# One norm moved ahead of a masking, and five small steps two units later, in a cross-attention and FFN kernel

## The chip, the cores and the metric

The kernel runs on one core of a Trainium2 chip. The metric is the device time of one execution in microseconds (us), lower is better. Engines are called as in the profile: PE (TensorE's matmuls), PEld (its weight loads), DVE (VectorE), ACT (ScalarE), POOL (GpSimd), SP (SyncE, which here only issues DMAs).

## The reference

What is computed, cut to what matters (one batch, 2048 tokens of width 256, a context of 1601 rows of width 192, 16 heads of width 64, one extra "null" key and value):

```python
x = x + _L0_xattn_ref(_layernorm(x, axis=-1), ctx_768, mask, g_norm, null_kv, Wq, Wkv, Wout, g_out)
x = x + _L0_ffn_ref(_layernorm(x, axis=-1), k0, k1, k2, s0, s1, s2)

def _L0_xattn_ref(x, context, mask, g_norm, null_kv, Wq, Wkv, Wout, g_out):
    q = layer_norm(x, g_norm) @ Wq
    k, v = jnp.split(context @ Wkv, 2, axis=-1)
    # 16 heads; null key and value in front; masked softmax; weighted values
    out = softmax(where(mask, (q * s) @ (k * s).T, -max)) @ v
    return layer_norm(out @ Wout, g_out)

def _L0_ffn_ref(x, k0, k1, k2, s0, s1, s2):
    h = s0 * (concat([x, -x]) @ where(k0, 1.0, -1.0))
    h = s1 * ((relu(h) * 2) @ where(k1, 1.0, -1.0))
    return s2 * ((relu(h) * 2) @ where(k2, 1.0, -1.0))
```

The signs and sizes of the scalars s0, s1, s2 are folded into the FFN's weights and its last scale.

## The kernel before, in words

The 2048 tokens are four blocks of 512 (`b`), the 16 heads are eight pairs (`p`). The attention is a list of 32 units `u`, one for each pair and block, pairs outermost; unit 0 is pair 0 with block 0, unit 1 is pair 0 with block 1. Everything is issued in the written order (a manual schedule): each engine takes its instructions in the order of the code, and waits by semaphore for what others make.

A unit has this course, with the names that the profile shows:

- A loop over 13 chunks of 128 keys (`KC`). For each, PE computes the scores `sT` (L393; L404 adds the shift for the first two), ACT makes the exponentials `e` (L406), and POOL adds them up in `acc` (L621, L623). In the same loop PE makes a chunk of coarse scores for the *next* unit, `max` (L356, L340), from `qr` and `kr`, and DVE takes its maximum, `mx` (L359, L343). `max` lies in the two PSUM buffers called flex (`ps_f`), so a chunk can be computed only when the maximum before the last one has been taken. `sT`, `av` and `po` use the two others (`ps_s`).
- At the loop's end DVE combines the maxima in `mcol` (L364).
- PE computes the weighted values `av` (L413) over the same 13 chunks. Behind its third chunk comes `divided` for the unit before: PE sums `acc` over the keys (`den`, L431), DVE takes the reciprocal and multiplies (`aoT`, L433 and L434).
- Behind it, in this order: ACT copies `av` to `avs` (L671); `max_turned` turns `mcol` on PE and makes the shift `mT` on DVE (L369, L371); `project_out` for the unit before (PE `po` L421, then DVE into `y_sb`, L424 or L426); `project_q` for the unit after next (`psq` L213, then `qr` and `qT` on ACT); and a part of the next pair's keys or values (`psk` L238 and L243, `kT` on ACT L249, `kr` on DVE L250; or `psv`).

In the first two units there is more. The input norm of blocks 0 and 1 is done ahead of unit 0; that of blocks 2 and 3 inside units 0 and 1. It has two parts. `input_root` and `input_normed` take the statistics of four tiles on DVE (L77, L78), the root on ACT (L443), the reciprocal (L447) and the negated mean `nm` (L140) on DVE, and then eight steps on ACT (L143, L144) into `y_sb`; behind them one ACT step loads the table for the exponentials again (`warm`). After `av`, `input_turned` turns the result on PE (`xT`, L458) and scales it into `xnT`, one half on ACT (L459), one on DVE (L463). `project_q` for unit 2 reads `xnT` of block 2.

In unit 0 only there are two further pieces, both on DVE. The first is the masking of the context: `ctx_a` and `ctx_b`, 128 x 1602 each, are multiplied by `keep` (L641), after an SP DMA has filled the lower half of `ctx_b` (L639). The first readers of the masked context are the `psk` matmuls at the end of unit 0. The second is the signs: five steps on tiles of one or two columns (L665 to L669) that make `sgn`, the absolute scales and `s_out`. `sgn` is read four units from the end, where the FFN's first weights `w0` are made (L655, L657), and `s_out` in the FFN.

POOL's sums and ACT's exponentials are tied by two one-element copies on ACT: `seen` (L608, L611). The second, ahead of a unit's third exponential, waits for the last `acc` of the unit before, and POOL's first sum of a unit stands behind it.

Of the kernel before, what the change touches and what calls it, by code (L numbers as in the profile page):

```python
# [12 lines left out]
AF = mybir.ActivationFunctionType  # L13
# [23 lines left out]
def xattn_ffn(ctx, tc, x, ctxT, mask, g_norm, null_kv, wq, wkv, wout, g_out, k0, k1, k2, s0, s1, s2, out):  # L37
    nc = tc.nc
# [20 lines left out]
    eps_sb = cp.tile([128, 1], F32, name="eps_sb")  # L59
# [8 lines left out]
    warm = cp.tile([128, 1], F32, name="warm")  # L68

    def stats(src, n, name, mv=None):  # L70

        at = 0 if mv is None else 2
        if mv is None:
            mv = sp.tile([128, 4, 2], F32, tag="mv", name=f"mv_{name}")
        for j in range(n):
            st = sp.tile([128, 6], F32, tag="st", name=f"st_{name}_{at + j}")
            nc.vector.bn_stats(st, src[:, j, :])  # L77
            nc.vector.bn_aggr(mv[:, at + j, :], st)  # L78
        return mv
# [8 lines left out]
    def centred(dst, src, mv, r, j):  # L88
        nc.vector.tensor_scalar(dst, src, mv[:, j, 0:1], r[:, j : j + 1], ALU.subtract, ALU.mult)  # L89
# [10 lines left out]
    def norm_begin(b, src, name):  # L100

        mv = stats(src[:, ts(b, 4), :], 4, f"{name}{b}")
        r = sp.tile([128, 4], F32, tag="rstd", name=f"rstd_{name}{b}")
        norms[b] = (mv, r)

    def norm_root(b):
        mv, r = norms[b]
        nc.scalar.activation(r, mv[:, :, 1], AF.Sqrt, bias=eps_sb)

    def norm_end(b, dst, src, beside=False):  # L110
        mv, r = norms[b]
        nc.vector.reciprocal(r, r)
        if beside:
            centred_beside(dst, src, mv, r, b)
            return
        for j in range(4 * b, 4 * b + 4):
            centred(dst[:, j, :], src[:, j, :], mv, r, j - 4 * b)
# [19 lines left out]
    def centred_beside(dst, src, mv, r, b):  # L137

        nm = sp.tile([128, 4], F32, tag="nm", name=f"nm_{b}_{n_slots}")
        nc.vector.tensor_scalar(nm, mv[:, :, 0], -1.0, None, ALU.mult)  # L140
        for j in range(4):
            t = 4 * b + j
            nc.scalar.activation(dst[:, t, :], src[:, t, :], AF.Identity, bias=nm[:, j : j + 1])  # L143
            nc.scalar.mul(dst[:, t, :], dst[:, t, :], r[:, j : j + 1])  # L144

    with ExitStack() as att:
# [293 lines left out]
        def input_root(b):  # L440
            mv = stats(x_sb[:, ts(b, 4), :], 4, f"x{b}")
            r = sp.tile([128, 4], F32, tag="rstd", name=f"rstd_x{b}")
            nc.scalar.activation(r, mv[:, :, 1], AF.Sqrt, bias=eps2_sb, scale=1.0 + EPS)  # L443
            return mv, r

        def input_normed(b, mv, r, beside=False):
            nc.vector.reciprocal(r, r)  # L447
            if beside:
                centred_beside(y_sb, x_sb, mv, r, b)
                return  # L450
            for j in range(4):
                centred(y_sb[:, 4 * b + j, :], x_sb[:, 4 * b + j, :], mv, r, j)
# [127 lines left out]
        with tc.manual_schedule():  # L580
            for u, (p, b) in enumerate(units):
# [48 lines left out]
                if u == len(units) - 2:  # L630
                    norm_begin(0, y_sb, "y")
                    norm_root(0)
                    norm_end(0, y_sb, y_sb, beside=True)

                    nc.scalar.activation(warm, eps_sb, AF.Exp)
                if u == 0:


                    nc.sync.dma_start(out=ctx_b[64:, 1:], in_=ctxT[128:CD, :])  # L639
                    for part in (ctx_a, ctx_b):  # L640
                        nc.vector.tensor_tensor(part, part, keep, ALU.mult)  # L641
                if u < 2:
                    input_normed(u + 2, *input_root(u + 2), beside=True)
                    nc.scalar.activation(warm, eps_sb, AF.Exp)

                av = spare(f"av_{p}_{b}")
                for k in range(KC):
# [3 lines left out]
                if u in (len(units) - 4, len(units) - 3):  # L651
# [4 lines left out]
                    else:  # L656
# [2 lines left out]
                        )  # L659
                        nc.vector.tensor_scalar_mul(s1b[:, 0:1], sgn[:, 1:2], 2.0)  # L660
                        nc.vector.tensor_scalar_mul(s1b[:, 1:2], sgn[:, 1:2], -1.0)
                if u == 0:


                    nc.vector.tensor_scalar(sgn, s_sb[:, 0:2], 0.0, None, ALU.is_ge)  # L665
                    nc.vector.tensor_scalar(sgn, sgn, 2.0, -1.0, ALU.mult, ALU.add)
                    nc.vector.tensor_tensor(s_sb[:, 0:2], s_sb[:, 0:2], sgn, ALU.mult)
                    nc.vector.tensor_scalar(s_out, s_sb[:, 0:1], s_sb[:, 1:2], 8.0, ALU.mult, ALU.mult)
                    nc.vector.tensor_tensor(s_out, s_out, s_sb[:, 2:3], ALU.mult)  # L669
# [166 lines left out]
```

## Time and profile before

| | |
|---|---|
| Median of 3 runs | 1310.03 us (1309.79 to 1311.21) |
| Profiled execution | 1309.9 us, span 1308.1 us, mean granted clock 0.996 |
| PE busy | 1290.2 us, 99% of the span |
| DVE busy | 819.7 us, 63% |
| ACT busy | 624.7 us, 48% |
| POOL busy | 997.9 us, 76% |
| Costliest group | POOL `acc` L623, 352 sums, 847.0 us |
| Unit 0's loop begins, unit 1's, unit 2's | about 39, 80.8, 115.4 us |

The span counts from the first to the last instruction. The granted clock is the share of TensorE's full speed that the chip allowed. A duration in the trace includes the time for which an instruction was held after it was issued, so that the same operation can have rows of different length. "Idle before" is the time for which an engine had nothing running ahead of an instruction, with what ended it.

### The profile page before, as it was taken

Reading aid. Unit: us, or ns where it says so; the run is one execution under the profiler, and the core shown is the slowest. Engines: PE = TensorE matmul, PEld = TensorE weight load, DVE = VectorE, ACT = ScalarE, POOL = GpSimd, SP = SyncE. Lnnn points to the kernel's source line nnn. Section 1 sums busy time; section 2 is a strip of 40 time slices with the busy share of each in tenths; the row PEclk is TensorE's granted clock in tenths of the full one; section 3 lists DMA queues with packets and bytes.
Section 4 is the critical chain, followed back from the end, with each engine's and each line's share of the span. In section 5 each row is a group of like instructions: output and inputs, shape, how many; then the busy total and the mean of one; then the engine's idle time right before and its main releaser. Section 6 shows DMA issues by size and latency. Waiting matters only on the chain.

```text
span 1308.1 us, 15963 instructions
## 1 busy us (share of the span) xinstructions
PE 1290.2 (99%) x6568; PEld 657.8 (50%) x6568; DVE 819.7 (63%) x822; ACT 624.7 (48%) x740; POOL 997.9 (76%) x503
## 2 busy tenths in 40 slices
PE   8989999999999999999999999999999999999998
PEld 6334444444444444444444444444444443688887
DVE  7877666666666666666666666666666784554431
ACT  4576444444444444454555555555555457321121
POOL 4768988898889888998889888988898999611100
PEclk9989999999999999999999999999999999999999
DMA  6100000000000000000000000000000010000000
GB/s 143 21 1 5 1 1 13 6 1 1 13 5 1 1 13 5 1 1 5 9 5 1 1 13 5 1 1 5 1 17 1 1 41 1 1 9 9 17 17 17
DMA packets 16122, 13.18 MB, mean 10 GB/s; under 512 B 2656, under 2 KB 15520, under 8 KB 16048
## 3 DMA queue, kind: packets, MB, share of 16 engines
q1 hardware_dynamic: 14928, 11.02, 3.2%
q8 instruction: 52, 0.85, 0.3%
q10 hardware_dynamic: 640, 0.79, 0.2%
q0 software_dynamic: 480, 0.34, 0.2%
q14 instruction: 22, 0.18, 0.0%
HBM read 10.04 MB, written 2.10 MB: 9 GB/s over the span
## 4 chain that ended last, share of the span: by engine, by line
PE 91%; DVE 3%; ACT 2%; POOL 2%; DMA 1%; issue 1%; SPq 0%; DVEq 0%; POOLq 0%; ACTq 0%
PE sT L393 28%; PE av L413 26%; PE ps L720 9%; PE max L356 7%; PE psq L213 4%; PE po L421 4%; PE ps L746 2%; PE den L431 2%; PE psv L298 2%; PE psk L238 2%; PE sT L404 1%; DVE mx L359 1%; POOL acc L623 1%; PE psv L310 1%; DMA x_sb<-in_x 1%; PE psk L243 1%
## 5 line engine op out<-in xcount | busy, mean ns | idle before, releaser
L623 POOL TENSOR_TENSOR acc<-acc,e 128x1024 f32<-128x1024 f32 (+1 forms) x352 | 847.0, 2406 | 27.6
L359 DVE TENSOR_REDUCE mx<-max 128x2 f32<-128x1024 f32 x384 | 452.0, 1221 | 81.4 <-PE max L356 81.3
L406 ACT ACTIVATE e<-sT,maskb 128x1024 f32<-128x1024 f32 (+1 forms) x416 | 459.6, 1113 | 42.0 <-PE sT L404 11.8
L393 PE MATMUL sT<-qT,kT 64*128 64x512 f32 (+1 forms) x1664 | 448.5, 612 | 0.8 <-ACT e L406 0.2
L413 PE MATMUL av<-e,v 128*64 128x512 f32 (+1 forms) x1664 | 369.5, 594 | 0.2 <-ACT e L406 0.2
L356 PE MATMUL max<-kr,qr 64*128 64x512 f32 x768 | 292.4, 750 | 0.0
L413 PEld LDWEIGHTS av<-e,v 128*64 128x64 f32 (+1 forms) x1664 | 116.7, 137 | 237.7 <-issue 222.6
L393 PEld LDWEIGHTS sT<-qT,kT 64*128 64x128 f32 (+1 forms) x1664 | 130.4, 181 | 153.6 <-ACT e L406 144.3
L671 ACT COPY avs<-av 128x512 f32<-128x512 f32 x32 | 18.7, 585 | 321.6 <-PE av L413 321.6
L433 DVE RECIPROCAL aoT<-den 128x512 f32<-128x512 f32 x31 | 104.0, 3356 | 60.0 <-PE den L431 60.0
L621 POOL TENSOR_TENSOR acc<-e,e 128x1024 f32<-128x1024 f32 x32 | 75.6, 2362 | 70.1 <-ACT seen L611 58.4
L356 PEld LDWEIGHTS max<-kr,qr 64*128 64x128 f32 x768 | 76.1, 187 | 90.4 <-DVE mx L359 68.4
L371 DVE TENSOR_TENSOR mT<-mt,pick 128x512 fp32r<-128x512 f32 x32 | 22.1, 691 | 119.0 <-PE mt L369 119.0
L720 PE MATMUL ps<-h0hi,w 128*128 128x512 f32 x256 | 79.6, 392 | 0.1
L720 PE MATMUL ps<-h0lo,w 128*128 128x512 f32 x256 | 78.9, 389 | 0.0
L122 POOL TENSOR_TENSOR y_sb<-y_sb,gout_sb 128x256 f32<-128x256 f32 x12 | 9.3, 776 | 88.8 <-DVE y_sb L89 88.8
L214 ACT ACTIVATE qr<-psq 128x512 fp32r<-128x512 f32 x32 | 19.1, 597 | 100.0 <-PE psq L213 97.1
L213 PE MATMUL psq<-xnT,wq 128*128 128x512 f32 x124 | 60.2, 609 | 2.5 <-DVE xnT L463 2.5
L709 DVE SCALAR_TENSOR_TENSOR h1lo<-ps,h1hi 128x1024 fp32r<-128x1024 f32 x16 | 19.6, 1224 | 68.3 <-ACT h1hi L708 68.2
L708 ACT ACTIVATE h1hi<-ps 128x1024 fp32r<-128x1024 f32 x16 | 16.4, 1025 | 95.0 <-PE ps L720 95.0
L421 PE MATMUL po<-wo,aoT 128*128 128x256 f32 x256 | 60.6, 379 | 0.0
L404 PE MATMUL sT<-mT,ones_r 64*128 64x512 f32 x128 | 52.3, 787 | 1.3 <-DVE mT L371 1.3
(157 smaller groups left out, 1060.9 us busy)
## 6 DMA issues: line engine op xcount, KB each, us to landing
out_x<-o SPq DMA_DIRECT2D x7, 256.0 KB, 2.1
x_sb<-in_x SPq DMA_DIRECT2D x3, 512.0 KB, 8.2
wa<-in_wkv SPq DMA_DIRECT2D x8, 128.0 KB, 2.7
wq<-in_wq SPq DMA_DIRECT2D x8, 128.0 KB, 2.2
wo<-in_wout SPq DMA_DIRECT2D x8, 128.0 KB, 2.0
xnT<-in_k SPq DMA_DIRECT2D x1, 1024.0 KB, 5.7
wb<-in_wkv SPq DMA_DIRECT2D x15, 64.0 KB, 2.4
ctx_a<-in_ctxT SPq DMA_DIRECT2D x2, 256.0 KB, 8.1
```

What stands on the lines that cost most here:

```text
L213: nc.tensor.matmul(ps[:, 0, :], weights[p][0][:, c, :], xnT[:, b, c, :], start=c == 0, stop=c == 1)
L356: nc.tensor.matmul(ps[:, j, :w], qr[rows, ts(t, 128)], kr[rows, ds(start, w)], start=True, stop=True)
L359: nc.vector.tensor_reduce(maxima[p, b][:, t, :, c], ps[:, :, :w], AX.X, ALU.max)
L393: nc.tensor.matmul(ps[:n, j, :], kT[rows, ds(128 * k, n)], qT[rows, :], start=k < 2, stop=k >= 2, skip_group_check=k >= 2,)
L404: nc.tensor.matmul(ps[:n, j, :], ones_r[rows, :n], mT[rows, :], start=False, stop=True)
L406: nc.scalar.activation(e[:n], ps[:n], AF.Exp, bias=maskb[:n, k : k + 1])
L413: nc.tensor.matmul(av[ts(j, DH), 0, :], v[:n, k, ts(j, DH)], e[:n, j, :], start=k == 0, stop=k == KC - 1)
L421: nc.tensor.matmul(pv[:, t, :], aoT[:, ts(t, 128)], weights[p][3], start=True, stop=True)
L433: nc.vector.reciprocal(aoT, ps)
L621: nc.gpsimd.tensor_tensor(acc, es[0], es[1], ALU.add)
L623: nc.gpsimd.tensor_tensor(acc[:m], acc[:m], es[k][:m], ALU.add)
L720: nc.tensor.matmul(ps[:, f, :], w(c)[:, ts(2 * g + f, 128)], parts[part][:, c, :], start=i == 0, stop=i == len(steps) - 1,)
```

## The change

In unit 0 the block of code with the norm (`input_root`, `input_normed` and the table step) and the one with the masking change places: the norm of the third block of tokens (block 2) now comes first, then the DMA and the two maskings. In unit 1 there is no masking, and nothing changes there. The five sign steps are made in unit 2 instead of unit 0, at the same place in the unit. No instruction is added or taken away; the numbers of instructions on each engine are the same.

```diff
@@ -633,15 +633,15 @@
                     nc.scalar.activation(warm, eps_sb, AF.Exp)
+                if u < 2:
+                    input_normed(u + 2, *input_root(u + 2), beside=True)
+                    nc.scalar.activation(warm, eps_sb, AF.Exp)
                 if u == 0:
                     nc.sync.dma_start(out=ctx_b[64:, 1:], in_=ctxT[128:CD, :])
                     for part in (ctx_a, ctx_b):
                         nc.vector.tensor_tensor(part, part, keep, ALU.mult)
-                if u < 2:
-                    input_normed(u + 2, *input_root(u + 2), beside=True)
-                    nc.scalar.activation(warm, eps_sb, AF.Exp)
 
                 av = spare(f"av_{p}_{b}")
@@ -659,7 +659,7 @@
-                if u == 0:
+                if u == 2:
                     nc.vector.tensor_scalar(sgn, s_sb[:, 0:2], 0.0, None, ALU.is_ge)
                     nc.vector.tensor_scalar(sgn, sgn, 2.0, -1.0, ALU.mult, ALU.add)
                     nc.vector.tensor_tensor(s_sb[:, 0:2], s_sb[:, 0:2], sgn, ALU.mult)
                     nc.vector.tensor_scalar(s_out, s_sb[:, 0:1], s_sb[:, 1:2], 8.0, ALU.mult, ALU.mult)
                     nc.vector.tensor_tensor(s_out, s_out, s_sb[:, 2:3], ALU.mult)
```

On DVE the order around the end of unit 0 becomes: `mcol`, eight statistics, reciprocal, `nm`, `ctx_a`, `ctx_b`, then `xnT`, `mT`, `kr`. In unit 2 the sign steps stand between the product `aoT` and `mT`. ACT, POOL, PE and SP keep their order.

## The prediction

> **What bounds the kernel now.** I read the page first, then the chain of waits around the end of the first unit, then the timelines of VectorE (DVE) and GpSimd (POOL) there, then windows cut at the edges where the granted clock changes.
>
> The page:
> ```profile
> span 1308.1 us, 15963 instructions
> PE 91%; DVE 3%; ACT 2%; POOL 2%; DMA 1%; issue 1%; SPq 0%; DVEq 0%; POOLq 0%; ACTq 0%
> ```
> TensorE (PE) carries 91% of the chain. So the change pays only where PE stands still, and what PE gains there stays gained unless a later wait takes it back.
>
> The chain of waits, columns start, length, what; the end of unit 0 first, and the same steps of unit 1 for comparison:
> ```profile
> 57.92 3.98 DVE ctx_b L641
> ...
> 64.07 0.30 ACT rstd_x L443
> 64.50 2.09 DVE nm L140
> ...
> 73.09 0.76 DVE xnT L463
> 73.90 3.78 PE psq L213 x4
> 77.68 2.25 PE psk L238 x4
> 79.93 0.87 PE psk L243 x4
> 80.80 0.86 PE sT L393 x4
> ...
> 111.45 1.72 PE psq L213 x4
> 113.16 1.35 PE psk L238 x4
> 114.51 0.87 PE psk L243 x4
> 115.38 0.86 PE sT L393 x4
> ```
> PE's last av matmul of unit 0 ends at 65.02 (timeline). After it the chain is not on PE until 73.90: it comes through the two maskings of the context, the norm of block 2, and xnT. Then psq and the first psk take 3.78 + 2.25 us, in unit 1 1.72 + 1.35.
>
> Windows of one clock period each; the last columns are clock, DMA share, GB/s:
> ```profile
> 34.99:38.40 3.41, 2.00 (x7) 0.44 (x5) 2.42 (x4) 1.08 (x2) 0.00 (x0) 1.00 0.55 98
> 65.71:69.12 3.41, 0.88 (x4) 0.40 (x4) 3.34 (x4) 2.41 (x6) 3.25 (x3) 1.00 0.00 0
> 69.12:72.53 3.41, 1.59 (x5) 0.79 (x5) 2.24 (x3) 3.35 (x7) 3.33 (x2) 0.50 0.00 0
> ```
> The clock halves at 69.12, after a window with PE busy 0.88 us of 3.41, and comes back at 79.36. A window with 2.00 busy did not halve it. The slow psq and psk are therefore a second cost of the same hole.
>
> DVE's timeline, and POOL's beside it:
> ```profile
> 55.11 2.88 DVE L641 TENSOR_TENSOR ctx_a<-ctx_a,keep 128x1602 f32<-128x1602 f32 x1
> 57.92 3.98 DVE L641 TENSOR_TENSOR ctx_b<-ctx_b,keep 128x1602 f32<-128x1602 f32 x1
> 64.50 2.08 DVE L140 TENSOR_SCALAR nm<-mv_x 128x4 f32<-128x4 f32 x1
> ```
> ```profile
> 56.39 3.82 POOL L623 TENSOR_TENSOR acc<-acc,e 128x1024 f32<-128x1024 f32 x1
> 60.29 3.84 POOL L623 TENSOR_TENSOR acc<-acc,e 128x1024 f32<-128x1024 f32 x1
> 71.49 2.33 POOL L623 TENSOR_TENSOR acc<-acc,e 66x1024 f32<-66x1024 f32 x1
> ```
> They take turns. ctx_a ends 1.68 us after a POOL sum ended (56.31), and ctx_b 1.69 us after the next (60.21); the sum that meets a masking takes 3.8 us instead of 2.36. nm, 0.14 us alone (its shortest row), ends with the POOL sum at 66.55.
>
> **The change, part by part.**
>
> *The norm goes ahead of the masking.* In the changed kernel's order the eight statistics stand right behind mcol, so they start at 55.11 instead of 61.82. They took 2.22 us (to 57.33), the root 0.30, the reciprocal 0.18; nm is issued at about 57.8. Alone it ends at 57.9; waiting for the sum begun at 56.39, at 58.8, which I take since every nm beside a running sum waited. ScalarE's (ACT) eight steps took 3.87 us (66.61 to 70.48) and the table load with the warm step 1.49: y is ready at 62.7 and ACT free at 64.2, both before av's end. So the norm costs PE nothing now; its cover is the av loop, with 2.3 us to spare.
>
> From av's end I take the steps from unit 1, where y was ready early too: av ended at 108.59, xnT on DVE ran from 110.37 to 111.12, psq's weights loaded at 111.17, that is 2.58 us later. Here: 65.02 + 2.58 = 67.60 against 73.90, a gain of 6.30 us.
>
> *The maskings go behind nm.* They need 1.68 us each and take turns with POOL. If ctx_a gets in ahead of the next sum they end at 64.4; if it waits for that sum (2.36) and ctx_b for the next, at 66.8. xnT is due on DVE at 65.02 + 1.78 = 66.80, and psk, the first reader, at 67.60 + 1.72 = 69.3. Both orders fit, the second with no slack; then a delay passes to xnT one for one. Their DMA (ctx_b's lower half, SP) keeps its place in SP's queue and was issued at 32.5, landing 4.4 us later.
>
> *The clock.* PE now idles from about 66.15 (transposes done) to 67.60. The window 65.71 to 69.12 then holds 0.44 + 1.52 = 1.96 us of PE work, next to the 2.00 that kept the clock and far from 0.88. So I take psq to sT at unit 1's 3.93 us (111.45 to 115.38) instead of 6.90 (73.90 to 80.80): a gain of 2.97. Together 9.27, and unit 1's sT starts at 71.53.
>
> *The sign steps leave unit 0 for unit 2.* Five small steps ran from 66.49 to 71.43, 4.94 us, two of them held by POOL; they were hidden, since xnT waited for ACT until 73.09. Left in place they would now stand between ctx_b and xnT and cost 2.5 to 4.9 us. In unit 2 they stand behind the product aoT (ends 139.07) and ahead of mT (143.47), where DVE idles 4.40 us. At 4.94 they end at 144.0; unheld about 0.8 us, and with a further wait of 2.4, at 146.4. Behind them wait mT, needed at 150.61, and the copy of po to y_sb (1.22 us), whose bank the next sT needs at 149.75: even the longer case ends at 148.4. Cost nothing. Readers of sgn come in the last units.
>
> *What is late next.* POOL is not sped up: two sums still meet a masking, so it ends unit 0 at 73.8 as before. The wait for it in unit 1 (seen, L611, 84.27) moves to 75.0: it holds, by 1.2 us. But the two kr steps (L250) move from 81.40 to 72.13, into POOL's last sum:
> ```profile
> L250 DVE SCALAR_TENSOR_TENSOR kr<-drop,nullk,kT x28: 628/634/639, 81.4 to 929.5; 128x401 fp32r<-128x401 uint8 x14, 128x400 fp32r<-128x400 uint8 x14
> ```
> None of the 28 ran beside POOL, so this row cannot price it. The nearest is w0 (L657), the same operation with a byte input and a float input: issued at 1051.75 beside sums, it took 4.45 us and ended 2.15 after the sum at 1054.05. So kr should wait until about 73.87. The Trainium skill, SBUF — State Buffer, section "Who interferes with whom", says that a VectorE instruction with two SBUF inputs contends with a GpSimd instruction that reads SBUF. By that rule kr waits too, a cost that the moved lines do not show; without it the sum would be the one with kr at no cost.
>
> Behind kr stands mx: both kr end at 74.9, the first mx (due 73.23) starts about 74.8 and ends at 76.05, and the second max chunk on PE, due at 84.52 - 9.27 = 75.25, needs the bank it frees: PE is late by 0.95, say 1.0 us. The loop has no room to win it back: mx starts follow each other by 1.14 to 1.20 us, with rows of 1.22. Bounds: nothing (kr not held) to 1.7 (a whole sum waited for).
>
> **Sum.** The profiled execution took 1309.9 us, 1.8 beyond its span and 0.1 under the median 1310.03. 1309.9 - 6.30 - 2.97 + 1.0 = 1301.6; on the median 1301.8. I say 1301.7. With kr's bounds 1300.6 to 1302.5.
>
> **Rivals.**
> 1. *kr is not held* (it wins the turn, or doesn't contend): 1309.9 - 9.27 = 1300.6, so 1300.7. For it: kr's 28 short rows, and a start only 0.6 us after the sum's. Against: w0 and both maskings waited.
> 2. *The clock halves all the same.* 1.96 is a little under 2.00. From 69.12 PE would run at half speed for up to the 10.24 us seen before and lose up to 5.1; kr, later, then misses POOL: 1309.9 - 9.27 + 5.1 = 1305.7. Against: 0.88 is much further away.
> 3. *The sign steps run late in unit 2.* If all five waited for a sum of 2.44 they would end at 151.3, and y_sb 1.9 later: sT is 3.4 late, 1305.0. Decides from an end past 147.8. Against: one of them (L668) ran beside a sum.
> 4. *Slower: POOL's lateness stays.* If POOL ran later against PE in every unit, each unit that makes keys would pay the kr wait. In the trace a kr starts only 1.15 us after POOL's last sum in units after the first two (217.78 against 216.63), so a lateness beyond 1.15 decides. 13 more pairs at 1.0: 1301.6 + 13 = 1314.6. Against: POOL starts every unit afresh behind the seen wait, and idles there (58.4 us over 23 waits).
> 5. *It doesn't do what it says*: another wait holds xnT as long as before, 1310. The chain shows none.
>
> **How the numbers follow.** Forecast 0.64; kr free 0.16; clock 0.09; late signs 0.05; slower 0.03; no change 0.03. 0.2% is 2.6 us, about what a measurement here can tell: the first four are faster (0.94). The range takes the first two with their bounds and reaches up to the late signs: 1300.0 to 1305.0; the clock case lies outside.
>
> **What the changed profile would show.** Stats at 55.1; maskings after 58.8, ended by 66.9; xT right behind av at 65.0; psq near 67.6 with 0.43 a matmul and the clock at 1.00 throughout; unit 1's sT near 71.5; the first kr near 1.7 to 2.4 us long instead of 0.64, and mx behind it; sign steps between aoT and mT of unit 2, with PE not waiting for mT. A clock of 0.50 after 69, maskings past 67, or later kr rows above 0.64 would make it wrong.

## The result, and the profile after

| | before | changed |
|---|---|---|
| Median, first comparison | 1309.91 us (1308.82 to 1311.21, 4 runs) | 1302.28 us (1301.98 to 1303.78, 4 runs) |
| Ratio, 95% interval | | 0.9942 (0.9927 to 0.9957) |
| Median, second comparison | 1310.19 us (1308.63 to 1311.27, 16 runs) | 1302.71 us (1301.84 to 1303.28, 5 runs) |
| Ratio, 95% interval | | 0.9942 (0.9930 to 0.9954) |
| Profiled execution, span | 1309.9, 1308.1 us | 1301.98, 1300.2 us |

The change makes the kernel faster by 0.58%, about 7.6 us. The page of the changed kernel, and its chain of waits from the end of unit 0 into unit 1's loop (start, length, what):

```profile
span 1300.2 us, 15963 instructions
PE 95%; DVE 2%; ACT 1%; POOL 1%; DMA 1%; issue 0%; DVEq 0%; POOLq 0%; ACTq 0%
```
```profile
53.85 11.31 PE av L413 x52
65.17 1.04 PE xT L458 x8
...
66.23 0.70 ACT xnT L459
...
66.95 0.76 DVE xnT L463
...
67.75 1.98 PE psq L213 x4
69.74 1.35 PE psk L238 x4
71.08 0.93 PE psk L243 x4
...
72.03 0.50 ACT kT L249
...
72.56 2.48 DVE kr L250 x2
75.04 1.15 DVE mx L359
...
76.23 0.50 PE max L356 x2
```

The transposes now follow av at once, psq starts at 67.75 instead of 73.90, and psq and the first psk run at the short durations. Then the chain leaves PE once more, for kr and mx. The same steps in PE's timeline, before and after (columns start, length, engine, line, and in brackets the idle time before with what ended it):

```profile
73.90 3.78 PE L213 MATMUL psq<-xnT,wq 128*128 128x512 f32 x4 [2.46 <-DVE xnT L463]
80.64 1.02 PE L393 MATMUL sT<-qT,kT 64*128 64x512 f32 x4
81.09 0.80 PE L404 MATMUL sT<-mT,ones_r 64*128 64x512 f32 x2
```
```profile
67.75 1.98 PE L213 MATMUL psq<-xnT,wq 128*128 128x512 f32 x4 [1.45 <-DVE xnT L463]
71.79 1.02 PE L393 MATMUL sT<-qT,kT 64*128 64x512 f32 x4
72.25 0.80 PE L404 MATMUL sT<-mT,ones_r 64*128 64x512 f32 x2
```

L404 adds the shift to a unit's first scores, so that its first start marks the beginning of a unit. In units 1, 2 and 3 it starts at 81.09, 115.67, 150.04 before and at 72.25, 107.55, 142.17 after. Unit 1 begins 8.84 us earlier, unit 2 8.12, unit 3 7.87, and the span ends 7.9 earlier: all of the gain is made in unit 0, and 0.72 and 0.25 us are given back in units 1 and 2. From unit 3 on, each unit takes the same time in both kernels within 0.02 us.

Timelines of the changed kernel, DVE and then POOL, unit 0 (start, length, engine, line):

```profile
57.94 0.97 DVE L140 TENSOR_SCALAR nm<-mv_x 128x4 f32<-128x4 f32 x1
58.82 1.81 DVE L644 TENSOR_TENSOR ctx_a<-ctx_a,keep 128x1602 f32<-128x1602 f32 x1
60.56 3.99 DVE L644 TENSOR_TENSOR ctx_b<-ctx_b,keep 128x1602 f32<-128x1602 f32 x1
72.56 2.48 DVE L250 SCALAR_TENSOR_TENSOR kr<-drop,nullk,kT 128x401 fp32r<-128x401 uint8 x2 [4.27 <-ACT kT L249]
```
```profile
58.96 3.90 POOL L623 TENSOR_TENSOR acc<-acc,e 128x1024 f32<-128x1024 f32 x1
62.94 3.83 POOL L623 TENSOR_TENSOR acc<-acc,e 128x1024 f32<-128x1024 f32 x1
71.70 2.35 POOL L623 TENSOR_TENSOR acc<-acc,e 66x1024 f32<-66x1024 f32 x1
```

ctx_a got in ahead of the sum at 58.96, the first of the two orders that the prediction left open; ctx_b waited for it. Two sums again meet a masking, so the last one runs from 71.70 to 74.06, and the first kr, issued at 72.56, ends 0.43 us after it at 74.49 (1.93 us long). What PE waits for, and the clock windows that hold the holes near 37 us and 67 us:

```profile
76.23 0.50 PE L356 MATMUL max<-kr,qr 64*128 64x512 f32 x2 [0.55 <-DVE mx L359]
```
```profile
34.85:38.26 3.41, 2.30 (x7) 0.55 (x6) 2.43 (x4) 1.09 (x2) 0.00 (x0) 1.00 0.60 116
65.57:68.98 3.41, 1.96 (x10) 1.17 (x9) 1.35 (x2) 0.92 (x2) 3.33 (x2) 1.00 0.00 0
```

The second window holds the hole: it has 1.96 us of PE work, and the clock stays at 1.00.

### The profile page after: what moved, and what is told of

Its sections match the earlier page's. It is cut to its first block, busy times and chain, and to the rows that moved or that the text cites. A ratio compares the mean times of both kernels' runs of the same rounds, so it can differ in the third digit from the quotient of the medians.

```text
span 1300.2 us, 15963 instructions
## 1 busy us (share of the span) xinstructions
PE 1286.8 (99%) x6568; PEld 656.4 (50%) x6568; DVE 820.0 (63%) x822; ACT 624.9 (48%) x740; POOL 998.2 (77%) x503
## 4 chain that ended last, share of the span: by engine, by line
PE 95%; DVE 2%; ACT 1%; POOL 1%; DMA 1%; issue 0%; DVEq 0%; POOLq 0%; ACTq 0%
PE sT L393 29%; PE av L413 28%; PE ps L720 10%; PE max L356 7%; PE po L421 4%; PE psq L213 4%; PE ps L746 2%; PE den L431 2%; PE psv L298 2%; PE psk L238 1%; PE sT L404 1%; PE psv L310 1%; PE psk L243 1%; PE max L340 1%; PE mt L369 1%; DMA gn_sb<-in_g_norm 1%
## 5 line engine op out<-in xcount | busy, mean ns | idle before, releaser
L404 PE MATMUL sT<-mT,ones_r 64*128 64x512 f32 x128 | 52.3, 788 | 1.2 <-DVE mT L371 1.2
```

Of the source, the lines that this page charges most:

```text
L404: nc.tensor.matmul(ps[:n, j, :], ones_r[rows, :n], mT[rows, :], start=False, stop=True)
```

## The experiments

The theory: the masking ahead of the statistics made a hole on PE, the hole halved the clock, and both go; the signs' move keeps DVE free for xnT; kr, now beside POOL's last sum, costs a little. The rivals are that one part alone does it, that psq was slow for another reason, and that kr's wait costs nothing.

**1. The swap alone**

```diff
 changed kernel
-                if u == 2:
+                if u == 0:
                     nc.vector.tensor_scalar(sgn, s_sb[:, 0:2], 0.0, None, ALU.is_ge)
```


> The norm ahead of the masking, the sign steps left in unit 0. Theory (the signs' move protects the gain): the five steps now start behind ctx_b at about 64.6 and, held by GpSimd's sums as in unit 2 of the changed kernel (7.2 us) or as before (4.9 us), end at 69.5 to 71.8; xnT follows, psq starts at 70.3 to 72.5 instead of 67.75, the hole is long enough to halve the clock again, and the time is 1306.3 to 1308.5 us. Rival (the signs do not matter): psq near 67.75 and the time near 1302.

Measured 1308.07 us against 1310.18, ratio 0.9989 (0.9980 to 0.9999). The timeline:

```profile
71.85 0.74 DVE L463 TENSOR_SCALAR xnT<-xT,gn_sb 128x512 f32<-128x512 f32 x1
72.65 3.78 PE L213 MATMUL psq<-xnT,wq 128*128 128x512 f32 x4 [6.03 <-DVE xnT L463]
```

The signs ran from 64.78 to 71.93 and xnT stood behind them. PE's wait ahead of psq is 6.03 us, against 1.45 in the changed kernel; a window held 0.35 us of work, and the clock was at 0.50 from 69.68 to 76.51. The swap alone is worth 2 us; the signs' move carries the rest.

**2. The signs alone**

```diff
 kernel before
-                if u == 0:
+                if u == 2:
                     nc.vector.tensor_scalar(sgn, s_sb[:, 0:2], 0.0, None, ALU.is_ge)
```


> The sign steps in unit 2, the norm still behind the masking. Theory (in the old order the signs lie hidden under ScalarE's eight steps): psq still at 73.9 with the clock at 0.50, and the time within 0.5 us of before, 1309.9 to 1310.4. Rival (the signs' move brings the gain): near 1302.

Measured 1309.70 us, ratio 0.9995 (0.9986 to 1.0005): no difference. psq started at 73.94 and took 3.78 us, and unit 2 took 34.64 us (L404 to L404) instead of 34.37. So neither half alone brings the gain, and the signs' new place costs 0.25 to 0.27 us.

**3. The masking left out of the kernel before**

```diff
 kernel before
-                    for part in (ctx_a, ctx_b):
-                        nc.vector.tensor_tensor(part, part, keep, ALU.mult)
```


> The kernel before without the two multiplications of the context by keep, which do nothing to these inputs since the mask is all ones and the null column is zero; norm and signs in their old places. Theory (the 6.9 us of masking ahead of the statistics are the hole): statistics at 55.1, psq at 67.7, clock 1.00, and, since no sum of GpSimd is held by a masking, its last sum of unit 0 ends near 70.8 instead of 74.06, so that kr is not held (rows of 0.64 us): span near 1299.2, time near 1301.2 us, about 1 us below the changed kernel. Rival (kr is late for another reason): kr long and the time near 1302.

Measured 1300.92 us, ratio 0.9931 (0.9916 to 0.9946), span 1298.8. In its timeline:

```profile
67.31 1.99 PE L213 MATMUL psq<-xnT,wq 128*128 128x512 f32 x4 [1.45 <-DVE xnT L463]
72.12 1.18 DVE L250 SCALAR_TENSOR_TENSOR kr<-drop,nullk,kT 128x401 fp32r<-128x401 uint8 x2 [4.26 <-ACT kT L249]
```

With norm and signs in their old places, taking the 6.9 us away ahead of the statistics gives the same psq: it starts 12.60 us after mcol (54.71), in the changed kernel 12.59. This kernel leaves out work, so it shows the cause and is no rival version. POOL's last sum ends before kr, kr is short, and unit 1 takes 34.58 us as in the kernel before, against 35.30 in the changed one.

**4. to 6. The clock alone**

Needless matmuls keep PE busy in the hole of the kernel before. The first try put 38 into the free half of av's bank:

```diff
 kernel before, unit 0, ahead of input_turned (20) and behind max_turned (18)
+                        nc.tensor.matmul(av[:, 1, :128], ident, ident, start=True, stop=True)
```


> The kernel before with 38 needless 128x128 matmuls added on TensorE in the hole of unit 0, 20 ahead of the transposes and 18 behind the turn of the maxima, into an unused half of av's bank. Theory (psq and psk were slow because the hole halved the clock): psq still starts at 73.9, the clock stays at 1.00, psq to sT takes about 4.2 instead of 6.9 us, and the time falls by 2.7 us to 1307.2. Rival (psq and psk are slow there for another reason, such as their operands' first use): they stay at 3.78 and 2.25 us, time 1309.9 to 1310.5.

Measured 1317.12 us, slower: the added matmuls waited for ACT's copy avs, which reads the same tile, and started only at 72.58. It tells nothing of the clock. The second put them into the tiles that the transposes use:

```diff
 kernel before, block 2 in input_turned, and unit 1's maxima in max_turned
+                for _ in range((20, 4, 4, 4)[j] if b == 2 else 0):
+                    nc.tensor.matmul(pt[:, 0, ts(j, 128)], ident, ident, start=True, stop=True)
...
+            for _ in range(18 if (p, b) == (0, 1) else 0):
+                nc.tensor.matmul(ps[:, 1, :128], ident, ident, start=True, stop=True)
```


> The kernel before with needless 128x128 matmuls in the hole of unit 0, now in the tiles xT (32 of them, ahead of and between the transposes) and mt (18), so that they need not wait for the copy of av. Theory (the hole halves the clock, and that alone slows psq and psk): psq still starts at 73.9, clock 1.00 throughout, unit 1's sT starts 2.6 to 2.9 us earlier, time near 1307.3 us. Rival (psq and psk are slow there for another reason): 1309.9 to 1310.5.

Measured 1310.71 us, ratio 1.0009 (1.0000 to 1.0018). The clock stayed at 1.00 and psq to sT took 3.94 us, but each matmul took 0.23 us, twice what I had counted, and psq started at 77.40. The third had half as many (10, 2 and 9):

> The kernel before with half as many needless matmuls in the hole of unit 0 (10 ahead of the transposes, 2 between each two, 9 behind the turn of the maxima), since each took 0.22 us and the 50 of the run before it pushed psq from 73.9 to 77.4. Theory (the halved clock alone makes psq and psk slow): psq starts at 73.9, clock 1.00, psq to sT takes 3.9 to 4.1 us instead of 6.74, unit 1's first L404 near 78.4 instead of 81.1, time near 1307.3 us. Rival (the gain of the warm clock is taken back later in unit 1): time 1309 to 1310.

Measured 1307.45 us against 1309.80, ratio 0.9982 (0.9973 to 0.9991). Its profiled execution ran the opening late: the clock was at 0.50 from 40.46 to 43.87, of which more in experiment 8, and mcol started at 57.03 instead of 55.01. ctx_a then took 1.83 us instead of 2.88, which gave 1.05 us back, so that a psq at 74.88 answers to 73.90 in the kernel before:

```profile
74.88 1.98 PE L213 MATMUL psq<-xnT,wq 128*128 128x512 f32 x4 [0.81 <-DVE xnT L467]
76.70 1.51 PE L238 MATMUL psk<-ctx_a,wa 128*128 128x401 f32 x4
```

psq to sT took 4.04 us instead of 6.74. So the halved clock, and not psq's operands, made these steps slow; by itself that is worth 2.4 us in the medians and 2.7 in the trace.

**7. kr from PSUM**

The changed kernel itself was run beside this and the next two (

> The changed kernel once more, as the base for the three runs beside it: 1302.0 us, 0.6% below before.

): 1302.71 us, unit 1 35.33 us. Four of its five executions (1302.60 to 1303.28 us) have a mean clock of 0.998 or 0.999; the fifth, the traced one, has 1.000 and took 1301.84. Experiment 8 shows a likely reason.

```diff
 changed kernel, project_k
                 nc.vector.scalar_tensor_tensor(
-                    kr[:, keys], drop[:, keys], nullk[:, 0:1], kT[:, keys], ALU.mult, ALU.add
+                    kr[:, keys], drop[:, keys], nullk[:, 0:1], ps[:, i, :w], ALU.mult, ALU.add
                 )
```


> The changed kernel with kr made from the PSUM bank psk instead of the copy kT, so that it has one SBUF tensor input instead of two. Theory (kr is held because both of its inputs lie in SBUF while GpSimd's sum reads SBUF): the first kr takes about 0.64 us though the last sum of unit 0 runs beside it, mx is not late, TensorE does not wait for the second max chunk, span 1299.4 and time 1301.3 us. Rival (kr waits for GpSimd whatever it reads, or the late mx costs nothing): first kr near 1.9 us or the time unchanged at 1302.

Measured 1307.32 us, 4.6 us slower than the changed kernel: neither theory had that. The first part held: beside the sum (72.61 to 74.97) the first kr took 0.63 us. But the end of unit 4 shows what came with it:

```profile
210.74 0.49 ACT L249 COPY kT<-psk 128x401 f32<-128x401 f32 x1 [1.17 <-PE psk L243]
211.27 0.63 DVE L250 SCALAR_TENSOR_TENSOR kr<-drop,nullk,psk 128x401 fp32r<-128x401 uint8 x1 [3.28 <-ACT kT L249]
211.94 0.49 ACT L249 COPY kT<-psk 128x401 f32<-128x401 f32 x1 [0.70 <-DVE kr L250]
212.47 0.63 DVE L250 SCALAR_TENSOR_TENSOR kr<-drop,nullk,psk 128x401 fp32r<-128x401 uint8 x1 [0.56 <-ACT kT L249]
```

ACT and DVE now read the same tile, and take turns by semaphore: ACT's second copy waits 0.70 us for DVE, and all exponentials stand behind it. Twelve units from unit 5 on take 0.31 to 0.35 us longer (34.05 against 33.71, 34.68 against 34.37), 3.8 us together. In units 1 and 2 the same price meets what the changed kernel pays there: unit 1 takes 34.92 us against 35.30, unit 2 34.68 against 34.62. In all that is 3.5 us, and the executions at a mean clock of 1.000 agree: 1305.47 and 1305.77 us against 1301.84 to 1302.39. The rest of the difference between the medians has another reason: nine of these eleven executions have a mean clock below 1.000, and the traced one among them has the halved clock in the opening that experiment 8 shows. The Trainium skill, PSUM — Partial Sum Buffer, section "PSUM bank collisions raise a hardware error", says that ScalarE and VectorE reading one bank (2 KiB a partition) and quadrant at once raise an error, and that reads of different banks run clean. Here ACT's second copy and the kr that it waits for read different halves of the tile, of 2 KiB a partition each. So this wait is not one that such a collision would ask for: it comes of the semaphores, which here go by the whole tile.

**8. The signs split**

```diff
 changed kernel, unit 2's sign steps
                     nc.vector.tensor_tensor(s_sb[:, 0:2], s_sb[:, 0:2], sgn, ALU.mult)
+                if u == 3:
                     nc.vector.tensor_scalar(s_out, s_sb[:, 0:1], s_sb[:, 1:2], 8.0, ALU.mult, ALU.mult)
```


> The changed kernel with the last two sign steps (s_out) in unit 3 instead of unit 2. Theory (mT comes 0.25 us too late behind five steps, since psv needs the bank that mT reads): in unit 2 the chain's psv takes 1.78 instead of 2.03 us and the time falls by 0.25 us, too little to see in the times but visible in the start of unit 3, near 141.6 instead of 141.9. Rival (the longer psv has another cause): it stays 2.03.

In the changed kernel, DVE's timeline in unit 2, and the chain there:

```profile
130.88 2.33 DVE L665 TENSOR_SCALAR sgn<-s_sb 128x2 f32<-128x2 f32 x1
...
133.44 2.20 DVE L667 TENSOR_TENSOR s_sb<-s_sb,sgn 128x2 f32<-128x2 f32 x1
...
135.92 2.15 DVE L669 TENSOR_TENSOR s_out<-s_out,s_sb 128x1 f32<-128x1 f32 x1
138.00 0.68 DVE L371 TENSOR_TENSOR mT<-mt,pick 128x512 fp32r<-128x512 f32 x1
```
```profile
138.76 2.03 PE psv L298 x16
```

Three steps are held by sums, and the five take 7.2 us. mT ends at 138.68; the weight load of psv, which writes the buffer that mT reads, starts behind it at 138.73 after 0.80 us of waiting, and psv takes 2.03 us in the chain, against 1.78 in the kernel before. With three steps in unit 2 the chain's psv takes 1.78 us and unit 2 34.36, as before. So the theory holds. The time does not show it (1302.71 us): this profiled execution lost 1.7 us elsewhere, in its opening:

```profile
36.08:39.49 3.41, 1.72 (x11) 0.74 (x9) 1.66 (x3) 0.94 (x3) 0.00 (x0) 1.00 0.22 47
39.49:42.91 3.42, 3.42 (x18) 1.96 (x16) 1.82 (x2) 2.08 (x2) 0.10 (x1) 0.50 0.00 0
```

PE waits in every one of these kernels near 37 us for the first maxima. Where the windows' edges fall differs from execution to execution; here one window held the whole hole, 1.72 us of work, and the next ran at half speed. Unit 0 took 35.1 us from L404 to L404 instead of 33.4. Of these 1.7 us unit 1 gave 0.71 back: it took 34.59 us instead of 35.30. PE came later to kr, which was issued at 74.20 and so met only the end of POOL's last sum (72.63 to 74.99), and PE did not have to wait for mx. So the price of the held kr depends on the opening: by this trace the halved clock there costs the changed kernel about 1 us in the end, not 1.7.

**9. Both together**

> kr from PSUM and the split sign steps together, on the changed kernel: the gains add to about 1.0 us, time near 1301.1, span near 1299.2. If either is taken back later, 1301.5 to 1302.

Measured 1306.56 us. Its traced execution has no halved clock in the opening, and its unit 1 took 34.93 us: the 0.72 of the held kr is gone, but the 0.35 of the turns is there, in this unit and in 13 later ones.

**10. The first kr alone from PSUM**

```diff
 changed kernel with split signs, project_k, behind the loop with both copies of kT
+            for i in range(2) if first else ():
+                keys = ds(start + i * w, w)
                 nc.vector.scalar_tensor_tensor(
...
+                    kr[:, keys], drop[:, keys], nullk[:, 0:1], ps[:, i, :w], ALU.mult, ALU.add
                 )
```


> The changed kernel with split sign steps, and only the first pair's kr (unit 0) made from PSUM, behind both ScalarE copies of kT; every later kr as before. Theory (kr from PSUM cost 0.33 us in each later key unit because the readers of one PSUM tile go one after the other, and it was not the loss of the held kr that failed to pay): unit 1 takes 34.6 to 34.8 us from its L404 to that of unit 2 instead of 35.3, later units are as in the changed kernel, span near 1299.3 and time near 1301.3 us where the clock stays at 1.00, and 1.7 us more in a run whose clock halves near 39 us. Rival (reading psk on VectorE is slow in itself): unit 1 stays at 34.9 or more.

Here `first` is true for pair 1's first half alone; every other kr stays in the loop and reads kT. Measured 1301.09 us (1300.55 to 1302.89), ratio 0.9935 (0.9923 to 0.9948), span 1299.3. The two kr take 1.18 us beside POOL's sum; unit 1 takes 34.67 us, unit 2 34.38. So kr's wait did cost PE 0.72 us, and 0.09 of it is left. Both engines still read the same tile, but all of ACT's reads now stand ahead of DVE's, and the turns are gone. This version is 1.2 to 1.6 us under the medians of the changed kernel; the intervals of the two ratios overlap, so the difference itself is shown by the unit times, 0.63 us in unit 1 and 0.23 in unit 2, not by the medians.

**11. The opening's hole filled**

```diff
 kernel of experiment 10, max_turned of unit 0
+            for _ in range(3 if (p, b) == (0, 0) else 0):
+                nc.tensor.matmul(ps[:, 0, :128], ident, ident, start=True, stop=True)
```


> The kernel of the first run of this set with three needless 128x128 matmuls ahead of the first turn of the maxima, in the hole near 37 us. Theory (a clock window with 1.73 us of TensorE work halves the clock for 3.4 us, and one with 1.95 does not; the phase of the windows differs from run to run): no run halves the clock near 39 us, the runs lie closer together and their median falls to 1301.0 us. Rival (the spread of the runs has another cause): spread of 1.5 us as before, median as without them.

Measured 1301.68 us, from 1301.31 to 1301.84 over 5 runs: the spread fell from 2.3 to 0.5 us, and the profiled execution kept its clock. PE now stands still for 1.38 us in the opening instead of 1.68, so that a window of 3.41 us holds at least 2.03 us of work wherever its edges fall, against 1.73. That fits the theory, but five executions can also miss the bad edges by chance. The three matmuls, however, took 0.94 us and pushed the turn of the maxima, which the end of the hole waits for, so that the median is no better than without them. The expected median was missed for the same reason as in the second try above.

## Why the prediction was right, and where its terms were off

Forecast 1301.7, measured 1302.28 and 1302.71; the way and the mechanism were right. The executions whose mean clock was 1.000 throughout, and so had no halved clock in the opening (experiment 8), took 1301.84 to 1302.39 us.

- *The hole.* 6.30 us were forecast; from mcol (55.01 and 55.16) to psq it is 6.30. The changed trace is 0.15 us later at mcol already, so 6.15 shows in it. Experiment 3 reaches the same psq another way.
- *The clock.* Kept, as forecast, at the 1.96 us of PE work that was worked out. The edges of the window were taken from the trace before, though they fall elsewhere in each execution; this did no harm, since PE stands still for only 1.45 us there and any window of 3.41 us then holds at least 1.96. That 1.96 would be enough was a judgement between two known windows, 0.88 and 2.00, and the later ones with 1.72 and 1.74 show that it was nearer the edge than the prediction gave it. The gain was 2.70 us (6.74 to 4.04 by PE's timeline), not 2.97: in unit 1, from which I took 3.93, psq follows other matmuls, while here it starts behind a hole and takes 1.98 instead of 1.72.
- *What is late next.* kr was held as forecast, 1.93 us against 0.64. The rule of the Trainium skill in SBUF — State Buffer, section "Who interferes with whom", that the prediction set beside w0's row agrees: two inputs in SBUF, held; one (experiments 7 and 10), not held. The price of the held kr was 0.72 us, not 1.0. I had put the second max chunk late by 0.95, though the two figures given for it (76.05 and 75.25) are only 0.80 apart; in the trace PE idled 0.55 there. That kr meets the sum at all depends on the opening (experiment 8).
- *The signs.* Here a step was wrong: "cost nothing". The five took 7.2 us, inside the bound of 7.3 (139.07 to 146.4), and I looked for mT's readers at 150.61 and y_sb's at 149.75. The first to wait was another: psv needs the buffer that mT reads. Cost 0.25 us.
- *Left out.* The halved clock near 39 us of some executions, which adds 1.7 us to unit 0 and, in the changed kernel, spares unit 1 0.71 (experiment 8); the kernel before, as it stands, was not traced with it. The trace before shows PE standing still for 0.42 and 1.26 us there, so that a window with the whole hole would hold 1.73 us, but not that this is too little.

The terms add up: 6.15 + 2.69 - 0.72 - 0.25 = 7.87, and the span fell by 7.9. Rival 1 (kr free) and rival 2 (clock) are refuted by the changed trace. Rival 3 names the step that was wrong, but its price was 0.25 us and not 3.4. Rival 4 is refuted by the later kr rows, all 0.63 to 0.64, and rival 5 by psq.

## What to carry to other kernels

When the bounding engine waits at one place, read what else that wait costs: here a hole of nine microseconds also halved the clock for ten, and about a third of the gain came from there. After moving work out of a wait, follow every instruction that now starts earlier to the unit that did not get faster, and price the collision. And before putting small steps into an engine's idle time, list the buffers that the next instruction of that engine holds, not only the values that it makes.

## What the runs showed of the hardware

- The stretches of one clock in these traces are multiples of 3.41 us (10.24 us before, 61.44 ahead of it), with edges that differ from execution to execution. In the openings and at the end of unit 0, windows of that length at full clock with 0.35, 0.88, 1.72 and 1.74 us of PE work were followed by half clock, those with 1.91 to 2.30 by full clock. Half clock lasted 3.41, 6.83 or 10.24 us, one, two or three windows; a window at half clock with 2.05 us of work (before, 72.53 to 75.95) was followed by another at half clock, and one that was busy throughout by full clock. PE's busy time is not the whole rule: at the end of experiment 11's kernel a window with 1.62 us (1294.44 to 1297.85) was followed by full clock. The Trainium skill, TensorE: Matmul & The Clock Gate, Part 1, has the clock fall after an idle window of about that length. Here it also fell after windows that were half busy: the measurement decides.
- kr, with one byte and one float input in SBUF, is held by a GpSimd sum to its end; read from PSUM it is not. Of the sign steps in the changed kernel L665 and L667 (two columns) and L669 (one column, from two tiles) were held, 2.15 to 2.33 us each; L668, which makes one column from scalars, took 0.21 us beside a sum, before as after.
